# Transposing the normalised input by VectorE blocks and DMAs instead of TensorE, with the rows of x dealt to partitions, in an attention and feed-forward block on one core

## The chip, the core and the metric

The kernel runs on one core of a Trainium2 chip. TensorE (PE in the profile) multiplies matrices, VectorE (DVE), ScalarE (ACT) and GpSimd (POOL) do the elementwise work, and SyncE (SP) does nothing but issue DMAs, one after the other in the order of the program. Each engine works through its own list of instructions in order, so an instruction that waits holds up all that stand behind it on that engine. The metric is the device time of one execution in microseconds. The chip is free for this program: one core, no other work.

## The reference

The input x has 16 batches of 512 tokens by 256 features, and everything is float32. Cut to what matters:

```python
xn = layernorm(x)                                # over the 256 features
q, k = rope(xn @ wq), rope(xn @ wk)              # 8 heads of 128
s = q @ k.T / 128, causal mask;  p = softmax(s)  # 512 x 512 in each head
attn = sum over heads of (p @ (xn @ wv)) @ wo
h = relu(s0 * [xn, -xn] @ sign(k0)) * 2          # 512 -> 1024, signs are +1 or -1
h = relu(s1 * h @ sign(k1)) * 2                  # 1024 -> 1024
ffn = s2 * h @ sign(k2)                          # 1024 -> 256
out = x + attn + ffn
```

## The kernel before

The work is cut into slots, one for each head of each batch: slot g belongs to batch b = g // 8 and head h = g % 8, and there are 128 of them, with one more in the end for the last leftovers. The order of TensorE's instructions is the order in which the program writes them; the other engines' lists are laid out by a scheduler when the kernel is built.

In slot g, TensorE projects q and k for the next head (`project_qk(g + 1)`), multiplies the four rows of score blocks of head g (`score_row`), and puts matmuls of the feed-forward network between these rows, so that the softmax of a row (mask and maximum on VectorE, exponential on ScalarE, scaling on GpSimd) has time to finish. It then adds the output projection of head g - 2 (`project_o`) and ends with the product of probabilities and values of head g - 1 (`attend`). The feed-forward layers run as `ffn0`, `ffn1` and `ffn2`, spread over the eight slots of a batch.

The probabilities have to be transposed before `attend` can use them. This is done without TensorE, in `turn(g, ...)`: VectorE transposes 32 x 32 blocks within their partitions into a tile z (line 314), and 16 DMAs, one for each pair of partition quarters, carry the blocks to the partitions where they belong, in tile pT (line 321). SyncE issues these 16 DMAs in every slot. `attend(g)` stands near the end of slot g + 1, and its matmuls (po, line 333) need all 16 to have landed. The tiles z and pT have two buffers each.

The normalised input xn has to be transposed as well, once for each batch, since q, k, v and the first layer need features on partitions. Before the change TensorE does this, in `transpose_xn`: eight transposes of 128 x 128 into PSUM (tile pxn, line 229), with copies by VectorE (line 230), and a split into a high and a low part for the first layer (`xh` on ScalarE, `xl` on VectorE). For batch b + 1 it runs in the slot of head 6 of batch b, four transposes after the first row of scores and four after the third. The layer normalisation for batch b + 1 is in the slot of head 4. The load of x for batch b + 1 (line 88, one DMA of 512 KB) and the store of batch b - 1 (line 375, two DMAs of 256 KB) are issued by SyncE in the slot of head 1 of batch b, ahead of that slot's 16 carries.

DMAs of SyncE and ScalarE share eight completion semaphores in turn, so each DMA waits in its queue until the one eight places earlier has landed.

The first slot (`first_slot`) has to wait for loads, for the scales and for the first layer's weights (`make_w0`). The last one (slot 128, in `slot_of_head_0`) has no scores left: only the rest of the feed-forward network, `project_o` and the last `attend`.

Of the kernel before, what the change touches and what calls it, by code (L numbers as in the profile page):

```python
# [22 lines left out]
def kernel(  # L23
# [36 lines left out]
    nc = tc.nc  # L60
# [24 lines left out]

    def load_x(b):
        t = xpool.tile([P, NT, M], F32, tag="x", name=f"x_{b}")
        nc.sync.dma_start(t, x[b].rearrange("(c p) m -> p c m", p=P))
        return t


    xs = {0: xpool.tile([P, NT, M], F32, tag="x", name="x_0")}
    for c in range(NT):
        (nc.scalar if c % 2 else nc.sync).dma_start(xs[0][:, c, :], x[0, ts(c, P), :])
    wv_sb = wpool.tile([P, NM, HD], F32, tag="wv", name="wv_sb")
# [3 lines left out]
    def load_w(engine, sb, w, h0, h1):  # L99
# [8 lines left out]

    k0_sb = [
        hpool.tile([P, 2, F0], U8, tag="h1h", name=f"k0_{c}", bufs=2) for c in range(NM)  # L110
    ]
    k1_sb = work.tile([P, NF0, F1], U8, tag="v", name="k1_sb")
    k2_sb = hpool.tile([P, NF1, M], U8, tag="h1l", name="k2_sb", bufs=2)
    wo_sb = wpool.tile([P, H, M], F32, tag="wo", name="wo_sb")
# [8 lines left out]
    for c in range(NM):  # L123
        nc.sync.dma_start(k0_sb[c], k0.rearrange("(i c p) f -> c p i f", p=P, c=NM)[c])
    load_w(nc.sync, wq_sb, wq, 2, H)
# [35 lines left out]
    def make_w0():  # L161
        for c in range(NM):
            kb = hpool.tile([P, F0], F32, tag="h0h", name=f"kb_{c}")
            nc.vector.tensor_scalar(kb, k0_sb[c][:, 1, :], sg_sb[:, 0:1], None, ALU.mult)
            nc.vector.scalar_tensor_tensor(  # L165
                w0_sb[:, c, :], k0_sb[c][:, 0, :], sg_sb[:, 0:1], kb, ALU.mult, ALU.subtract
            )
# [49 lines left out]

    def transpose_xn(b):
        xn = xns.pop(b)
        xnT = npool.tile([P, NM, T], F32, tag="xnT", name=f"xnT_{b}")  # L220
        xh = npool.tile([P, NM, T], F32R, tag="xh", name=f"xh_{b}")
        xl = npool.tile([P, NM, T], F32R, tag="xl", name=f"xl_{b}")
        xnTs[b], halves[b] = xnT, (xh, xl)
        ready = []
        for m in range(NM):
            pool, tag = (ps_t, "t") if b else (ps_s, "s")
            pt = pool.tile([P, T], F32, tag=tag, name=f"pxn_{b}_{m}")
            for c in range(NT):
                nc.tensor.transpose(pt[:, ts(c, P)], xn[:, c, ts(m, P)], ident)  # L229
            nc.vector.tensor_copy(xnT[:, m, :], pt)  # L230
            if b == 0 and m == NM - 1:
                make_scales()
            ready.append(pt)
            if b or m:
                for n, pt in enumerate(ready, m + 1 - len(ready)):
                    nc.scalar.activation(xh[:, n, :], pt, AF.Identity, scale=c_sb)
                    nc.vector.scalar_tensor_tensor(
                        xl[:, n, :], xnT[:, n, :], c_sb, xh[:, n, :].bitcast(F32),
                        ALU.mult, ALU.subtract,
                    )  # L240
                ready.clear()
            yield

    Q = 32
    NQ = P // Q
    NB = NT * (NT + 1) // 2  # L250
    vts, qks, probs, pTs, oTs = {}, {}, {}, {}, {}
# [4 lines left out]
    def project_v(b, g):  # L256
        xnT = xnTs[b]
        vt = work.tile([P, NT, VH * D], F32, tag="v", name=f"v_{b}_{g}")
        vts[b, g] = vt
        for c in range(NT):  # L260
            pv = ps_mm.tile([P, T], F32, tag="mm", name=f"pv_{b}_{g}_{c}")
            for m in range(NM):
                nc.tensor.matmul(  # L263
                    pv, xnT[:, m, ts(c, P)], wv_sb[:, m, ts(g, VH * D)],
                    start=(m == 0), stop=(m == NM - 1),
                )
            nc.scalar.copy(vt[:, c, :], pv)
            yield

    def project_qk(g):  # L270
        b, h = divmod(g, H)
        res = []
        for name, w in (("q", wq_sb), ("k", wk_sb)):
            pq = ps_mm.tile([P, T], F32, tag="mm", name=f"p{name}_{b}_{h}")
            for m in range(NM):
                nc.tensor.matmul(  # L276
                    pq, w[:, m, ts(h, D)], xnTs[b][:, m, :],
                    start=(m == 0), stop=(m == NM - 1),
                )

            sw = work.tile([P, T], F32, tag="sw", name=f"sw{name}_{b}_{h}")
            nc.scalar.copy(sw[0:HALF, :], pq[HALF:D, :])  # L282
            nc.scalar.copy(sw[HALF:D, :], pq[0:HALF, :])  # L283
            rt = work.tile([P, T], F32, tag=f"{name}T", name=f"{name}T_{b}_{h}")
            nc.vector.tensor_tensor(rt, pq, cos_sb, ALU.mult)  # L285
            nc.gpsimd.tensor_tensor(sw, sw, sin_sb, ALU.mult)  # L286
            nc.gpsimd.tensor_tensor(rt, rt, sw, ALU.add)
            res.append(rt)
        qks[g] = res
# [18 lines left out]
    def turn(g, after):  # L308

        zs = work.tile([P, NQ, NB, Q], F32, tag="z", name=f"z_{g}")
        for ic, p in enumerate(probs.pop(g)):
            behind(nc.vector.transpose(  # L314
                zs[:, :, block(ic, 0) : block(ic + 1, 0), :].rearrange("p j c a -> p c j a"),
                p.rearrange("p (c j a) -> p c j a", j=NQ, a=Q),
            ), after)
        pT = work.tile([P, NQ, NB, Q], F32, tag="pT", name=f"pT_{g}")
        for i in range(NQ):
            for j in range(NQ):  # L320
                nc.sync.dma_start(pT[ts(j, Q), i, :, :], zs[ts(i, Q), j, :, :])  # L321
        pTs[g] = pT

    def attend(g):
        if not 0 <= g < N_SLOTS:
            return
        b, h = divmod(g, H)
        vt, pT = vts[b, h // VH], pTs.pop(g)
        po = ps_t.tile([P, T], F32, tag="t", name=f"po_{g}")

        for jc in range(NT):
            for ic in range(jc, NT):
                nc.tensor.matmul(  # L333
                    po[:, ts(ic, P)], vt[:, jc, ts(h % VH, D)], pT[:, :, block(ic, jc), :],
                    start=(jc == 0 and ic == 0), stop=(jc == ic), skip_group_check=True,
                )
        oT = work.tile([P, T], F32, tag="oT", name=f"oT_{g}")
        nc.vector.tensor_copy(oT, po)
        oTs[g] = oT
# [29 lines left out]
    def store(b):  # L369
        assert y_done[b] == [N_Y] * NT  # L370
        xt = xs.pop(b)
        for i in range(NT // 2):
            rows = xt[:, 2 * i : 2 * i + 2, :]
            nc.vector.tensor_tensor(rows, rows, ys[b][i], ALU.add)
            nc.sync.dma_start(
                out[b, 2 * i * P : 2 * (i + 1) * P, :].rearrange("(c p) m -> p c m", p=P),
                rows,
            )

# [3 lines left out]
    def ffn0(b, f):  # L383
# [5 lines left out]
        for c in range(NM):  # L389
            for i in range(2):  # L390
                nc.tensor.matmul(  # L391
                    ph, w0_sb[:, c, ts(f, P)], halves[b][i][:, c, :],
                    start=(c == 0 and i == 0), stop=(c == NM - 1 and i == 1),
# [8 lines left out]
    def ffn1(b, f):  # L402
        ph = ps_mm.tile([P, T], F32, tag="mm", name=f"ph1_{b}_{f}")
        for c in range(NF0):
            for i in range(2):
# [4 lines left out]
                if c < NF0 - 1 or i == 0:  # L410
                    yield
        hi = hpool.tile([P, T], F32R, tag="h1h", name=f"h1h_{b}_{f}", bufs=2)
        lo = hpool.tile([P, T], F32R, tag="h1l", name=f"h1l_{b}_{f}", bufs=2)
        nc.scalar.activation(hi, ph, AF.Relu)
# [28 lines left out]
    def first_slot():  # L443
        l0 = [ffn0(0, f) for f in range(NF0)]
        project_qk(1)
        pv = project_v(0, 0)
        next(pv)
        next(pv)
        for ic in range(NT):
            reduced, raised = score_row(0, ic)  # L450
            rest(l0[ic])
            next(pv, None)
        turn(0, reduced)
# [4 lines left out]
    def slot_of_head_0(g):  # L458

        b = g // H  # L460
        if b < B:
            l0 = [ffn0(b, f) for f in range(NF0)]
            project_qk(g + 1)
        else:
            l0 = [iter(())] * NF0
        last = ffn2(b - 1, NF1 - 1)
        for ic in range(NT):
            if b < B:
                reduced, _ = score_row(g, ic)
            if ic == 0:  # L470
# [3 lines left out]
            else:  # L474
                rest(l0[ic - 2])
        if b < B:
            turn(g, reduced)
        project_o(g - 2)
# [29 lines left out]
    def slot(g):  # L508
# [3 lines left out]
        tile = ffn1(b, h - 1)  # L512
        turned = transpose_xn(b + 1) if h == H - 2 and b + 1 < B else iter(())
        for ic in range(NT):
# [3 lines left out]
            else:  # L518
                some(tile, 4)
            if ic % 2 == 0:  # L520
                next(turned, None)
        turn(g, reduced)
        project_o(g - 2)
        rest(tile)
# [4 lines left out]
        if b + 1 < B:  # L529
            if h == H - 4:  # L530
                layernorm(b + 1, reduced)
            if h == H - 1:
                rest(project_v(b + 1, 0))

    def xs_next(b):
        if b < B:
            xs[b] = load_x(b)

    with tc.manual_schedule(engines={mybir.EngineType.PE}):
        with tc.manual_schedule(engines={mybir.EngineType.DVE}):  # L540
            scale_wq(nc.gpsimd, 0, 2, layernorm(0))
            rest(transpose_xn(0))
            project_qk(0)
            make_w0()
        first_slot()
# [54 lines left out]
```

## Time and profile before

| What | Value |
|---|---|
| Median of three runs | 2207.32 us (2206.61 to 2210.01) |
| The profiled execution | 2207.65 us, of which the span of its instructions 2205.8 us |
| TensorE busy | 2182.0 us (99% of the span), 9856 matmuls |
| VectorE busy | 1195.6 us (54%) |
| GpSimd, ScalarE busy | 950.5 us (43%), 868.7 us (39%) |
| DMAs that carry z to pT | 2048, of 40.0 KB, 1.9 us from issue to landing (median) |

The busy share says which engine has work nearly all the time. The chain of waits says what the end of the program was waiting for, step by step backwards. The list of waits says which engine stood idle for which other one. SyncE computes nothing, so it has no row among the busy engines: its time is seen in the timeline of its queue (rows marked SPq), where a row gives start, length and number of merged DMA issues.

### The profile page before, as it was taken

How to read it: one execution, taken by the hardware profiler on the slowest of the kernel's cores; microseconds unless marked ns; L12 is line 12 of the kernel's file. 1: busy time of each engine (PE TensorE's matmuls, PEld its weight loads, DVE VectorE, ACT ScalarE, POOL GpSimd, SP SyncE). 2: the span in 40 equal slices, each digit the busy share in tenths (PEclk: the TensorE clock that was granted, in tenths of full speed). 3: DMA queues.
4: the chain of work that ended last, by engine and by line, in shares of the span. 5: the costliest groups of instructions: out<-in, count | busy, mean ns of one | idle time of the engine just before them, and what ended most of it. 6: DMA issues, size and time to landing. Idle time of an engine off the chain costs nothing.

```text
span 2205.8 us, 30324 instructions
## 1 busy us (share of the span) xinstructions
PE 2182.0 (99%) x9856; PEld 1561.9 (71%) x9856; DVE 1195.6 (54%) x2993; ACT 868.7 (39%) x1959; POOL 950.5 (43%) x1067
## 2 busy tenths in 40 slices
PE   7999999999999999999999999999999999999998
PEld 4677777777777777776777777777667777777766
DVE  6555655556555565554655555555555645556544
ACT  4334333344434344344343433443333443433432
POOL 4443534435343353434534354353443534435342
PEclk9999999999999999999999999999999999999999
DMA  4112111121111211112111121111211111121111
GB/s 150 42 43 56 43 51 46 38 56 48 51 42 37 57 46 56 40 39 57 46 53 43 38 57 46 53 41 36 56 48 55 37 46 48 46 56 40 43 43 51
DMA packets 121676, 109.28 MB, mean 50 GB/s; under 512 B 35248, under 2 KB 120240, under 8 KB 121520
## 3 DMA queue, kind: packets, MB, share of 16 engines
q1 hardware_dynamic: 120384, 106.57, 18.0%
q8 instruction: 79, 1.29, 0.3%
q10 hardware_dynamic: 1136, 0.79, 0.1%
q14 instruction: 77, 0.63, 0.1%
HBM read 14.94 MB, written 8.39 MB: 11 GB/s over the span
## 4 chain that ended last, share of the span: by engine, by line
PE 97%; SPq 1%; DVE 1%; ACT 1%; issue 0%; POOL 0%; DMA 0%; POOLq 0%; ACTq 0%
PE ph L406 21%; PE y L356 15%; PE po L333 13%; PE s L295 12%; PE pv L263 10%; PE pq L276 10%; PE pk L276 10%; PE ph L391 5%; SPq L321 1%; PE pxn L229 1%; DMA pT<-z 0%; DMA x<-in_L_attn_x_dram 0%; DVE z L314 0%; DVE w_sb L165 0%; DVE h0l L399 0%
## 5 line engine op out<-in xcount | busy, mean ns | idle before, releaser
L286 POOL TENSOR_TENSOR swq<-swq,sin_sb 128x512 f32<-128x512 f32 x128 | 165.5, 1293 | 969.3 <-ACT swq L283 969.3
L406 PE MATMUL ph<-h0h,w_sb 128*128 128x512 f32 x1024 | 517.5, 505 | 0.0
L301 ACT ACTIVATE p<-s,nmax 128x128 f32<-128x128 f32 (+3 forms) x512 | 270.6, 529 | 361.1 <-DVE nmax L298 326.5
L406 PE MATMUL ph<-h0l,w_sb 128*128 128x512 f32 x1024 | 408.7, 399 | 0.0
L295 PE MATMUL s<-kT,qT 128*128 128x128 f32 (+3 forms) x1024 | 360.7, 434 | 1.9 <-ACT p L301 1.9
L304 POOL TENSOR_SCALAR p<-p,rl 128x128 f32<-128x128 f32 (+3 forms) x512 | 269.4, 537 | 200.7 <-DVE rl L303 199.1
L285 DVE TENSOR_TENSOR qT<-pq,cos_sb 128x512 f32<-128x512 f32 x128 | 88.6, 692 | 461.7 <-ACT swq L283 461.6
L333 PEld LDWEIGHTS po<-pT,v 128*128 128x128 f32 x2560 | 306.2, 192 | 19.9 <-PE ph L406 6.1
L333 PE MATMUL po<-pT,v 128*128 128x128 f32 x2560 | 308.4, 276 | 5.8 <-DMA pT<-z 4.4
L314 DVE STREAM_TRANSPOSE z<-p 128x128 f32<-128x128 f32 (+3 forms) x512 | 234.2, 490 | 68.2 <-POOL p L304 67.5
L298 DVE TENSOR_REDUCE nmax<-s 128x1 f32<-128x128 f32 (+3 forms) x512 | 251.5, 491 | 13.2
L295 PEld LDWEIGHTS s<-kT,qT 128*128 128x128 f32 x1024 | 182.7, 189 | 89.0 <-issue 62.0
L406 PEld LDWEIGHTS ph<-h0h,w_sb 128*128 128x128 f32 x1024 | 193.0, 188 | 73.2 <-issue 26.9
L406 PEld LDWEIGHTS ph<-h0l,w_sb 128*128 128x128 f32 x1024 | 193.2, 189 | 72.7 <-issue 26.8
L276 PE MATMUL pq<-xnT,wq_sb 128*128 128x512 f32 x512 | 242.6, 596 | 0.0
L356 PE MATMUL y<-wo_sb,oT 128*128 128x256 f32 x1024 | 241.8, 379 | 0.0
L276 PE MATMUL pk<-xnT,wk_sb 128*128 128x512 f32 x512 | 240.6, 592 | 0.0
L263 PE MATMUL pv<-wv_sb,xnT 128*128 128x512 f32 x512 | 227.2, 596 | 0.0
L356 PEld LDWEIGHTS y<-wo_sb,oT 128*128 128x128 f32 x1024 | 192.6, 189 | 29.7
L282 ACT COPY swq<-pq 64x512 f32<-64x512 f32 x128 | 74.6, 583 | 329.0 <-PE pq L276 327.4
L276 PEld LDWEIGHTS pk<-xnT,wk_sb 128*128 128x128 f32 x512 | 97.4, 190 | 123.0 <-issue 122.5
L296 DVE TENSOR_TENSOR s<-s,causal 128x128 f32<-128x128 f32 x512 | 150.3, 294 | 56.5 <-PE s L295 56.5
(61 smaller groups left out, 2519.9 us busy)
## 6 DMA issues: line engine op xcount, KB each, us to landing
pT<-z SPq DMA_DIRECT2D x2048, 40.0 KB, 1.9
out_dram<-x SPq DMA_DIRECT2D x32, 256.0 KB, 2.2
x<-in_L_attn_x_dram SPq DMA_DIRECT2D x15, 512.0 KB, 3.9
wv_sb<-in_L_attn_wv_dram SPq DMA_DIRECT2D x2, 512.0 KB, 9.3
k_sb<-in_L_ffn_k_dram SPq DMA_DIRECT2D x1, 1024.0 KB, 10.8
wo_sb<-in_L_attn_wo_dram SPq DMA_DIRECT2D x1, 1024.0 KB, 10.7
wq_sb<-in_L_attn_wq_dram SPq DMA_DIRECT2D x1, 768.0 KB, 6.8
wk_sb<-in_L_attn_wk_dram SPq DMA_DIRECT2D x1, 768.0 KB, 8.4
```

The lines of the kernel that those rows point to most:

```text
L263: nc.tensor.matmul(pv, xnT[:, m, ts(c, P)], wv_sb[:, m, ts(g, VH * D)], start=(m == 0), stop=(m == NM - 1),)
L276: nc.tensor.matmul(pq, w[:, m, ts(h, D)], xnTs[b][:, m, :], start=(m == 0), stop=(m == NM - 1),)
L286: nc.gpsimd.tensor_tensor(sw, sw, sin_sb, ALU.mult)
L295: nc.tensor.matmul(ps[:, :n], qT[:, ts(ic, P)], kT[:, :n], start=True, stop=True)
L296: nc.vector.tensor_tensor(ps[:, ts(ic, P)], ps[:, ts(ic, P)], causal, ALU.add)
L298: reduced = nc.vector.tensor_reduce(nmax, ps[:, :n], AX.X, ALU.max, negate=True)
L301: raised = nc.scalar.activation(p, ps[:, :n], AF.Exp, bias=nmax, accum_out=l)
L304: nc.gpsimd.tensor_scalar(p, p, rl, 1.0, ALU.mult, ALU.mult)
L314: behind(nc.vector.transpose(zs[:, :, block(ic, 0) : block(ic + 1, 0), :].rearrange("p j c a -> p c j a"), p.rearrange("p (c j a) -> p c j ...
L333: nc.tensor.matmul(po[:, ts(ic, P)], vt[:, jc, ts(h % VH, D)], pT[:, :, block(ic, jc), :], start=(jc == 0 and ic == 0), stop=(jc == ic), s ...
L356: nc.tensor.matmul(ys[b][c // 2][:, c % 2, :], lhsT[:, ts(c, P)], rhs, start=(y_done[b][c] == 0 and c % 2 == 0), stop=(y_done[b][c] == N_Y ...
L406: nc.tensor.matmul(ph, w1_sb[:, c, ts(f, P)], h0s[b][i][:, c, :], start=(c == 0 and i == 0), stop=(c == NF0 - 1 and i == 1),)
```

## The change

For batches 1 to 15, xn is transposed in the way the probabilities are: VectorE transposes 32 x 32 blocks into a tile zx (four instructions, which take a buffer of z's tag), and 16 DMAs on SyncE's queue carry them into xnT, which now has two buffers (`carry`, shared with `turn`). This is issued in the slot of head 4, after that slot's `turn`; the layer normalisation moves from head 4 to head 3, and the split into xh and xl becomes two instructions over all of xnT in the slot of head 6 (`split_xn`). Only batch 0 still uses TensorE's transposes.

So that a chunk of 128 tokens still comes out in order, row 32c + a of each 128 rows of x is put on partition a of a quarter, at place c. Loads of x and stores of out are therefore four DMAs of 128 KB, each to or from 32 partitions. Matmuls that need the other order of tokens (ffn0 reads xh and xl, VectorE's copy into oT) read or write in runs of 32 elements.

In SyncE's list the four loads of x for batch b + 1 now stand behind the first four of the 16 carries of pT in the slot of head 1, and ahead of the other twelve. The 16 carries of xnT stand between the carries of pT of heads 4 and 5.

In the first slot all four chunks of v are projected before the scores, and one of the two multiplications of `make_w0` moves to ScalarE. In the last slot the second half of ffn2 runs before `attend` instead of after it. The tiles h1h, h1l and oT have one buffer instead of two. The core of the diff:

```diff
-    def load_x(b):
+    def rows_of(t, b, i):
+        return t[b, ts(i, P), :].rearrange("(c a) m -> a c m", a=Q)
+
+    def load_x(b, engines):
         t = xpool.tile([P, NT, M], F32, tag="x", name=f"x_{b}")
-        nc.sync.dma_start(t, x[b].rearrange("(c p) m -> p c m", p=P))
+        for i in range(NQ):
+            engines[i % len(engines)].dma_start(t[ts(i, Q)], rows_of(x, b, i))
...
     def make_w0():
...
-            nc.vector.tensor_scalar(kb, k0_sb[c][:, 1, :], sg_sb[:, 0:1], None, ALU.mult)
+            nc.scalar.activation(kb, k0_sb[:, c, 1, :], AF.Identity, scale=sg_sb[:, 0:1])
...
+    def carry(to, blocks):
+        for i in range(NQ):
+            for j in range(NQ):
+                nc.sync.dma_start(to[ts(j, Q), i], blocks[ts(i, Q), j])
...
+    def transpose_xn(b, after):
         xn = xns.pop(b)
+        zx = work.tile([P, NQ, NM, NT, Q], F32, tag="z", name=f"zx_{b}")
+        for c in range(NT):
+            behind(nc.vector.transpose(
+                zx[:, :, :, c, :].rearrange("p j m a -> p m j a"),
+                xn[:, c, :].rearrange("p (m j a) -> p m j a", j=NQ, a=Q),
+            ), after)
+        new_xnT(b)
+        carry(xnTs[b], zx)
...
+    def split_xn(b):
...
+        nc.scalar.activation(
+            xh.rearrange(flat), xnTs[b].rearrange(flat), AF.Identity, scale=c_sb
+        )
+        nc.vector.scalar_tensor_tensor(
+            xl.rearrange(flat), xnTs[b].rearrange(flat), c_sb,
+            xh.rearrange(flat).bitcast(F32), ALU.mult, ALU.subtract,
+        )
...
     def store(b):
...
-            nc.sync.dma_start(
-                out[b, 2 * i * P : 2 * (i + 1) * P, :].rearrange("(c p) m -> p c m", p=P),
-                rows,
-            )
+        for i in range(NQ):
+            nc.sync.dma_start(rows_of(out, b, i), xt[ts(i, Q)])
...
     def ffn0(b, f):
...
-                    ph, w0_sb[:, c, ts(f, P)], halves[b][i][:, c, :],
+                    ph, w0_sb[:, c, ts(f, P)], tokens_by_row(halves[b][i], c),
...
     def slot_of_head_0(g):
...
+        if b == B:
+            rest(ffn1(b - 1, NF1 - 1))
+            project_o(g - 2)
+            rest(ffn2(b - 1, NF1 - 2), last)
+            attend(g - 1)
+            return
...
     def slot(g):
...
-        turned = transpose_xn(b + 1) if h == H - 2 and b + 1 < B else iter(())
...
         turn(g, reduced)
+        if h == H - 4 and b + 1 < B:
+            transpose_xn(b + 1, reduced)
...
-            if h == H - 4:
+            if h == H - 5:
                 layernorm(b + 1, reduced)
+            if h == H - 2:
+                split_xn(b + 1)
```

## The prediction

> **What bounds the kernel now.** I read the page's busy row and chain of waits first, then TensorE's waits, then the timelines of TensorE and SyncE's queue around the lines that change.
>
> ```profile
> PE 2182.0 (99%) x9856; PEld 1561.9 (71%) x9856; DVE 1195.6 (54%) x2993; ACT 868.7 (39%) x1959; POOL 950.5 (43%) x1067
> PE 97%; SPq 1%; DVE 1%; ACT 1%; issue 0%; POOL 0%; DMA 0%; POOLq 0%; ACTq 0%
> ```
>
> TensorE has work all the time and is 97% of the chain, so a matmul taken out of its list is time taken out of the kernel, and so is any wait put into it. Its waits are few (columns: total, times, longest):
>
> ```profile
> PE pxn L229 <- DVE xn L211: 7.5, 1, 7.5
> PE po L333 <- DMA pT<-z: 4.4, 3, 2.5
> PE ph L391 <- DVE w_sb L165: 2.4, 1, 2.4
> ```
>
> The second row matters most: po has waited for the carries three times, so they are near the edge. How near, the timeline of SyncE's queue tells, at heads 1, 4 and 5 of batch 1 (one window each; start, length, count):
>
> ```profile
> 192.65 10.02 SPq L321 DMA_DIRECT2D pT<-z  x16
> ...
> 240.21 10.01 SPq L321 DMA_DIRECT2D pT<-z  x16
> ...
> 254.40 10.01 SPq L321 DMA_DIRECT2D pT<-z  x16
> ```
>
> One set of 16 carries holds SP for 10.0 us, 0.63 us from issue to issue. A plain slot lasts 14.2 us (254.40 - 240.21): SP is busy for 70% of it, though SP has no row among the busy engines. The last carry lands 1.3 us after its issue ends (1.9 us from its start). TensorE needs those sets here:
>
> ```profile
> 254.08 2.39 PE L333 MATMUL po<-pT,v 128*128 128x128 f32 x20
> ...
> 269.15 1.05 PE L333 MATMUL po<-pT,v 128*128 128x128 f32 x8
> ```
>
> Head 4's set lands at 240.21 + 10.01 + 1.3 = 251.5, 2.6 us ahead of its po; head 5's at 265.7, 3.4 ahead. For head 1 the set lands at 204.0 and po starts at 204.62: 0.6 us. In between SP waits for VectorE's z, 738.0 us over 127 sets, so its list is never ahead: all the slack of a set is what I just worked out.
>
> **The change part by part.**
>
> *TensorE's transposes go.* In the chain they stand twice in the slot of head 6:
>
> ```profile
> 125.33 0.44 PE pxn L229 x4
> ...
> 128.70 0.44 PE pxn L229 x4
> ```
>
> 0.88 us a batch, 15 batches: -13.2 us. Batch 0 keeps its eight.
>
> *VectorE and ScalarE.* Removed per batch: two xnT copies (682 ns each), two xl (753), two xh (688). Added: four transposes of 128x256 (407 ns, the row of z<-p of that shape), one xl and one xh of 128x1024, about twice the 128x512 ones. VectorE ends 0.3 us up per batch, on an engine 54% busy. Two zx transposes stand ahead of head 4's last z transpose, in the place where two BN statistics (405 ns) stood before, and the first z of that set left on time. xh and xl follow h1h and oT at the end of head 6, where ScalarE waits 2.6 us for pq (327.4 us over 125 times) and VectorE about as long for swq. If that cover were gone, head 7's mask and exponential would be up to 1.3 us late and the third score row would wait for a PSUM buffer. I cost this at nothing.
>
> *The 16 carries of xnT on SP.* They are the same kind as pT's: SBUF to SBUF, 32 partitions, one run each (1 KB instead of 1.25 KB). No row shows them, so bounds: from above pT's 0.63 us per issue; from below the issues of x at the start, two in 0.88 us, 0.44 each. I take 0.63, as the row of the same kind; 40 KB and 32 KB differ less than 512 KB and 256 KB do, both of which took 380 ns. Head 4's set ends at 250.2, xnT's at 260.2, and only then can head 5's start, at z's 254.40 before. It ends at 270.2 and lands at 271.5. TensorE without the transposes is at po by 269.15 - 0.88 = 268.3. Stall 3.3 us, 15 times: +49.5 us. (At 0.44: 7.0 us for the set, 3.0 less, stall 0.3.) Behind that po stand head 6's last matmuls and all of head 7; head 6's own set starts 0.5 to 1 us late and has 2 us, and TensorE is itself late by then. Nothing gives the stall back, since z follows TensorE.
>
> Here the Trainium skill speaks the other way: "DMA: Bandwidth & Descriptors", section "Issuing engines are not separate DMA queues", says that the time a sequencer needs to initiate a DMA is usually small relative to the DMA itself. With that, sixteen carries with two slots to land in cost nothing, and the sum would be 2207.65 - 13.2 = 2194. The rows say 0.63 us of issue against 1.9 us to landing, and 10.0 of each 14.2 us. I follow the rows.
>
> *The clock after a stall.* At the end of before, po follows an idle of 2.48 us:
>
> ```profile
> 2195.16 3.91 PE L333 MATMUL po<-pT,v 128*128 128x128 f32 x20 [2.48 <-DMA pT<-z]
> ```
>
> The same 20 take 2.39 us above; the granted clock was 0.50 there for 3.41 us. An idle of 1.9 us (at 47.8) brought none. With 3.3 us I expect it about four times in five: half of 3.41 is 1.7 us lost, so 1.3 on average, 15 times: +19.5 us. Bounds: 0 and 1.7 each.
>
> *x and out in four DMAs.* Four loads of x come between the fourth and fifth carry of head 1, in the 14 batches 1 to 14. Each issue 0.38 us (a whole x or out) to 0.63 (a carry); I take 0.45, near the 0.44 of 128 KB loads. 1.8 us against 0.6 us of slack: stall 1.2 us (0.9 to 1.9), 14 times: +16.8 us, too short for the clock. The stores (four for two) fall before z at 192.65, where SP has been idle since 189: nothing. What they would wait for has landed by then.
>
> *Strided reads.* po reads pT in runs of 32 elements: its 20 passes take 2.23 us in the chain, 0.11 each, as long as a pass of s over dense columns (0.22 for two). So I cost runs of 32 at nothing for q, k, v. ffn0's passes are twice as fast per column (0.23 us for 512 against 0.43), and no row has runs at that rate: between 0 and, if the rate halved, 32 passes x 0.23 x 16 = +119 us. I take 0, the nearest row.
>
> *First and last slot.* Each normalisation now needs all four loads: +0.6 us. v before the scores fills TensorE while w0 is made, but waits for qT of head 1 behind w0 on VectorE; I put the gain against the 2.4 us wait at 1.5. At the end, `last` moves into the 2.48 us idle, which gives up to 1.6 us, but the final project_o then waits 0.75 us for oT uncovered, h1h has to wait for its single buffer, and the store has four issues, not two (+1.35). Both ends together -1, between -3 and +2. Single buffers elsewhere: ffn2 has read h1 and project_o has read oT, earlier in the same slot, before the next write.
>
> Sum: -13.2 + 49.5 + 19.5 + 16.8 - 1 = +71.6. The profiled execution took 2207.65 us (span 2205.8 and 1.85 around it), 0.3 above the median: 2279.
>
> **The rivals.**
>
> *Cheap issues, loads still late.* At 0.44 us per carry head 5 loses 0.3 us and no clock: -13.2 + 4.5 + 16.8 - 1 = +7, 2215. For: HBM loads of 128 KB issue that fast. Against: all 2048 carries, least 507 ns.
>
> *Nothing late, faster.* If SP's price is set by size or destination so that 16 carries take under 6.7 us (0.42 each) and four loads under 0.6 us beyond the slack, TensorE keeps only its gain: 2207.65 - 13.2 - 1 = 2193. It decides at the edge of po's slack: head 5's set must be issued by 256.9. For: TensorE bounds all else. Against: 10.0 us in every set.
>
> *Runs of 32 halve ffn0.* 2279 + 119, up to 2398; a tenth of it already leaves the range.
>
> **How the numbers follow.** Likeliest, SP's queue as priced: 0.78, 2279 (its own range 2245 to 2306: stall 2.7 to 3.8, clock 0 to 1.7, loads 0.9 to 1.9). Cheap issues 0.08, nothing late 0.09, ffn0 0.05. The range 2230 to 2306 reaches to carries at 0.5 us (stall 1.3, no clock: +22). Two runs of this kernel are told apart at about 0.2%. Faster 0.10 (nothing late, and a sliver of cheap issues), same 0.03 (the rest of cheap issues near zero), slower 0.87.
>
> **What would show it.** pxn down to 16 records; carries of xnT at SPq, ten microseconds a batch; the row of po waiting for pT at 60 to 80 us in some 30 waits instead of 4.4 in 3, half at head 5, half at head 1; granted clock 0.5 after head 5's; TensorE's busy sum up where po runs slow. It is wrong if that row stays at 4.4, if xnT's set takes much less than 10 us, or if ffn0's mean leaves 456 and 394 ns.

## The result, and the profile after

The changed kernel takes 2319.64 us (median of six runs, 2316.38 to 2328.72) against 2207.32 us: 1.0514 times as long, with a 95% interval of 1.0493 to 1.0535. It is 112 us slower, where 72 had been forecast. The profiled execution of it took 2324.51 us, with a span of 2322.5 us.

The page's busy row and chain of waits:

```profile
PE 2210.6 (95%) x9736; PEld 1568.0 (68%) x9736; DVE 1192.3 (51%) x3005; ACT 868.6 (37%) x1945; POOL 943.4 (41%) x1067
...
PE 74%; SPq 15%; DMA 3%; ACT 3%; issue 2%; DVE 2%; POOL 1%; ACTq 0%; DVEq 0%; POOLq 0%
```

TensorE has 120 matmuls fewer and is busy for 28.6 us more: its matmuls run slower in places. SP's queue, 1% of the chain before, is now 15% of it. TensorE's waits (total, times, longest):

```profile
PE s L322 <- ACT p L328: 66.6, 16, 5.0
PE po L356 <- DMA pT<-z: 23.8, 15, 2.3
PE pxn L260 <- DVE xn L216: 9.3, 1, 9.3
```

The second row was expected at 60 to 80 us in some 30 waits. It is there, but only for head 1. The first row was not expected. Before the change it was

```profile
PE s L295 <- ACT p L301: 1.9, 1, 1.9
```

and it is now a wait of about 4.3 us in each of 15 batches. SP's queue around head 1 of batch 1, and then around heads 4 and 5:

```profile
197.00 2.42 SPq L231 DMA_DIRECT2D pT<-z  x4
199.60 1.87 SPq L97 DMA_DIRECT2D x<-in_L_attn_x_dram  x4
201.51 7.71 SPq L231 DMA_DIRECT2D pT<-z  x12
```

```profile
246.34 10.01 SPq L231 DMA_DIRECT2D pT<-z  x16
256.45 10.04 SPq L231 DMA_DIRECT2D xnT<-zx  x16
266.60 10.03 SPq L231 DMA_DIRECT2D pT<-z  x16
```

SP does what was worked out: four loads of x take 1.87 us, sixteen carries of xnT take 10.04 us, and head 5's set starts late, right after them. The transfers themselves are no slower. The page's row of DMA issues for pT reads the same before and after, 1.9 us from issue to landing:

```profile
pT<-z SPq DMA_DIRECT2D x2048, 40.0 KB, 1.9
```

While SP issued the carries of xnT back to back (256.5 to 266.5), the core's 16 DMA engines were busy for 0.20 of the time (mean). So it is the issuing that fills up, not the DMA engines. But TensorE is not at po when this set lands. It stands earlier in the same slot, at a score row. The timelines of ScalarE, VectorE and TensorE there (the number in brackets is the engine's idle time before the row, with what ended it):

```profile
267.85 1.15 ACT L269 ACTIVATE xh<-xnT,c_sb 128x1024 fp32r<-128x1024 f32 x1 [6.83 <-DMA xnT<-zx]
...
269.04 1.28 DVE L272 SCALAR_TENSOR_TENSOR xl<-xnT,c_sb,xh 128x1024 fp32r<-128x1024 f32 x1 [5.75 <-DMA pT<-z]
...
272.06 0.91 PE L322 MATMUL s<-kT,qT 128*128 128x384 f32 x2 [3.54 <-ACT p L328]
...
279.79 2.39 PE L356 MATMUL po<-pT,v 128*128 128x128 f32 x20
```

The split of xn is written at the end of head 6's slot, but the scheduler put xh and xl at its beginning: xh stands in ScalarE's list right behind h1h of the feed-forward tile that the slot of head 5 computes. So ScalarE waits there 6.83 us for the last carry of xnT (issued by 266.49, landed at 267.7). The copies of q and k for head 7 and the exponentials of head 6 are queued behind xh, and the masks and maxima behind xl on VectorE. The third score row needs a PSUM buffer that the first one's exponential has to release, and TensorE waits. By the time po is reached, at 279.79, head 5's set has been there since 277.9. (The row of xl names pT, but xl waits for all eight DMA semaphores and for xh, and starts when xh ends.)

After such a wait TensorE runs at half clock. Windows before, in and after it (the column ahead of DMA's share is the granted clock):

```profile
262.00:268.00 6.00, 6.00 (x28) 3.95 (x28) 0.69 (x1) 0.15 (x1) 0.00 (x0) 1.00 0.21 55
268.60:272.00 3.40, 0.00 (x0) 0.00 (x0) 2.93 (x5) 3.17 (x7) 1.64 (x2) 1.00 0.25 65
273.30:276.50 3.20, 3.20 (x7) 1.81 (x6) 1.10 (x6) 0.89 (x4) 3.12 (x5) 0.50 0.25 64
```

In the whole trace the clock stood at half for 95.8 us, against 9.7 before. I count half of the time that TensorE was busy in these stretches as lost: 38.9 us against 3.2.

### The profile page after: what moved, and what is told of

It reads as the page before. It is cut to its first block, busy times and chain, and to the rows that moved or that the text cites. A ratio compares the mean times of both kernels' runs of the same rounds, so it can differ in the third digit from the quotient of the medians.

```text
span 2322.5 us, 30675 instructions
## 1 busy us (share of the span) xinstructions
PE 2210.6 (95%) x9736; PEld 1568.0 (68%) x9736; DVE 1192.3 (51%) x3005; ACT 868.6 (37%) x1945; POOL 943.4 (41%) x1067
## 4 chain that ended last, share of the span: by engine, by line
PE 74%; SPq 15%; DMA 3%; ACT 3%; issue 2%; DVE 2%; POOL 1%; ACTq 0%; DVEq 0%; POOLq 0%
PE ph L430 15%; SPq L231 14%; PE y L382 10%; PE po L356 10%; PE s L322 10%; PE pv L290 10%; PE pq L303 7%; PE pk L303 7%; PE ph L415 5%; DMA pT<-z 1%; DMA xnT<-zx 1%; SPq L97 1%; POOL swq L313 1%; ACT p L328 1%; ACT xh L269 1%
## 5 line engine op out<-in xcount | busy, mean ns | idle before, releaser
L430 PE MATMUL ph<-h0h,w_sb 128*128 128x512 f32 x1024 | 533.0, 521 | 0.0
L322 PE MATMUL s<-kT,qT 128*128 128x128 f32 (+3 forms) x1024 | 380.5, 454 | 66.6 <-ACT p L328 66.6
L430 PE MATMUL ph<-h0l,w_sb 128*128 128x512 f32 x1024 | 416.2, 406 | 0.0
L356 PEld LDWEIGHTS po<-pT,v 128*128 128x128 f32 x2560 | 307.6, 193 | 42.4 <-issue 31.6
L322 PEld LDWEIGHTS s<-kT,qT 128*128 128x128 f32 x1024 | 188.6, 195 | 160.0 <-ACT p L328 77.5
L430 PEld LDWEIGHTS ph<-h0h,w_sb 128*128 128x128 f32 x1024 | 199.0, 194 | 80.0 <-issue 33.9
L430 PEld LDWEIGHTS ph<-h0l,w_sb 128*128 128x128 f32 x1024 | 198.3, 194 | 78.2 <-issue 33.2
```

The costliest lines, as they stand in the source:

```text
L322: nc.tensor.matmul(ps[:, :n], qT[:, ts(ic, P)], kT[:, :n], start=True, stop=True)
L356: nc.tensor.matmul(po[:, ts(ic, P)], vt[:, jc, ts(h % VH, D)], pT[:, :, block(ic, jc), :], start=(jc == 0 and ic == 0), stop=(jc == ic), s ...
L430: nc.tensor.matmul(ph, w1_sb[:, c, ts(f, P)], h0s[b][i][:, c, :], start=(c == 0 and i == 0), stop=(c == NF0 - 1 and i == 1),)
```

## The experiments

All ratios are to the kernel before, measured beside it on the same chip.

**The split late.** The theory was that two costs lie on top of each other at head 6: the split placed too early, and behind it the late set of pT. The rival, B, was that the early split is all. The edit ties both instructions to the last score row of head 6: `behind(a, b)` keeps instruction a behind b in the scheduler's list. Cuts in the diffs are marked with dots.

```diff
-        nc.scalar.activation(
+        behind(nc.scalar.activation(
             xh.rearrange(flat), xnTs[b].rearrange(flat), AF.Identity, scale=c_sb
-        )
+        ), raised)
...
-                split_xn(b + 1)
+                split_xn(b + 1, reduced, raised)
```

> Only the split into xh and xl is tied to the last score row of head 6, so that ScalarE and VectorE do not stand before it while the carries of xnT land. Theory A (two costs lie on top of each other at head 6: the split placed too early stalls the score rows, and behind it the set of pT of head 5 is late because SP issues xnT first): the wait of s for p (66.6 us in the changed kernel) falls to near 0 and the wait of po for pT at head 5 appears, 3.3 us a batch, 15 times, with half clock after about four of five: 2207 - 13 + 50 + 20 + 21 (loads at head 1) = 2285 us. Rival B (the early split is the only cost at head 6, pT of head 5 is in time as in the changed kernel, where it had 2.0 us of slack): 2207 - 13 + 21 = 2216 us.

Measured: 2328.64 us (2325.56 to 2330.11), ratio 1.0553 (1.0535 to 1.0571). TensorE's waits, the largest and that of s:

```profile
PE po L356 <- DMA pT<-z: 87.3, 30, 4.6
...
PE s L322 <- ACT p L328: 1.9, 1, 1.9
```

The wait of s is gone, and that of po at head 5 has taken its place: idle time ahead of it is 63.9 us in 15 batches, as much as the 64.7 us of the wait that went. The late set of head 5 is a cost of its own, which the early split had only covered; rival B falls. The median is 9 us above that of the changed kernel, but the spans of the two profiled executions differ by 1.1 us (2322.5 and 2323.6), so this difference is not traced. Theory A's own figure, 2285, was too low. Both sizes in it were too small: 4.3 us a batch, not 3.3, and more time at half clock (104.7 us, 42.0 us lost). The row of po shows that the clock costs more than one window:

```profile
280.06 4.61 PE L356 MATMUL po<-pT,v 128*128 128x128 f32 x20 [3.54 <-DMA pT<-z]
```

All 20 run at half speed, and the windows after it still show 0.50 up to 285: two windows of 3.4 us, not one. In eleven of the 15 batches half clock lasted 6.8 us.

**The loads of x moved, with the split late.** In addition, the loads are issued in the slot of head 2.

```diff
     def slot_of_head_1(g):
...
-            xs_next(b + 1)
...
     def slot(g):
...
         turn(g, reduced)
+        if h == 2:
+            xs_next(b + 1)
```

> The split late as in the run before, and the loads of x moved from the slot of head 1 to that of head 2, where SP idles about 11 us. Both theories: the wait of po at head 1 (20.8 us above before, with little loss of clock) goes, so 21 to 25 us under the run before: 2263 us by theory A, 2194 us by rival B. If the loads were not what makes head 1 late, no difference.

Measured: 2296.61 us, ratio 1.0407 (1.0391 to 1.0422), 32 us under the run before. The row of po falls from 87.3 us in 30 waits to 64.4 in 16. The idle time ahead of po at head 1 falls from 22.3 to 3.7 us, and 42.0 us lost to the clock become 33.9. So the move gives more than the 21 to 25 us that were expected, because the clock counts with these waits too: three of the first run's stretches at half clock followed waits of 2.1 to 2.2 us at head 1, and here none does.

**Only the loads of x moved**, in the changed kernel, with the split where the scheduler had it.

> The changed kernel with only the loads of x moved to the slot of head 2. Loads as the cause at head 1: 20.8 us of waits go, and some half-clock windows after the longer ones: 2294 to 2299 us; the 12.0 us that a set of head 1 takes on SP falls to 10.0. Otherwise 2320.

Measured: 2297.77 us, ratio 1.0409 (1.0393 to 1.0424), 21.9 us under the changed kernel, as expected: idle time ahead of po at head 1 goes from 22.9 to 2.6 us, and a set of head 1 takes 10.02 us again. With the loads away, it makes no clear difference (2296.61 and 2297.77, in ranges that overlap) whether TensorE waits at the score row or at po.

**Carries of xnT by ScalarE.** The split late, the loads at head 2, and the 16 carries taken off SP: eight at the end of the slot of head 4 and eight at the end of head 5.

```diff
-        carry(xnTs[b], zx)
+    def carry_xn(b, quarters, after):
+        for i in quarters:
+            for j in range(NQ):
+                behind(nc.scalar.dma_start(xnTs[b][ts(j, Q), i], zxs[b][ts(i, Q), j]), after)
```

> As the second run (split late, loads at head 2), and the 16 carries of xnT issued by ScalarE, eight at the end of the slot of head 4 and eight at the end of head 5, so that SP issues pT alone. Theory A: pT of head 5 is in time and nothing stalls: 2207 - 13 = 2194 us, 69 us under the second run; if eight issues of 0.63 us do not fit into ScalarE's 3.4 us of idle time at the end of a slot, up to 1.6 us twice a batch, 2194 to 2242. Rival B: the same as the second run, 2194.

Measured: 2228.08 us, ratio 1.0096 (1.0080 to 1.0111), 68.5 us under the second run. The wait of po for pT is down to 1.1 us, once. Clock losses are back at 3.4 us. What is left is a wait of s (1.9 us of it was there before), and ScalarE's timeline shows where it comes from:

```profile
PE s L329 <- ACT p L335: 22.7, 16, 2.2
```

```profile
242.56 5.30 ACTq L259 DMA_DIRECT2D xnT<-zx  x8
247.98 0.58 ACT L316 COPY swq<-pq 64x512 f32<-64x512 f32 x1 [5.77 <-DMA xnT<-zx]
```

Eight issues hold ScalarE for 5.30 us, longer than its idle time there, and the score rows of head 5 are late by 20.8 us in 15 batches. DMA issues block ScalarE's list as they block SP's.

**Carries on both queues.** Four on SP and four on ScalarE in each of heads 4 and 5 (the scheduler put all eight of SP ahead of head 5's set). The diff is against the run before.

```diff
-            carry_xn(b + 1, (0, 1) if h == H - 4 else (2, 3), raised)
+            i = 2 * (h - (H - 4))
+            carry_xn(b + 1, nc.sync, i)
+            carry_xn(b + 1, nc.scalar, i + 1, raised)
```

> As the run with all carries on ScalarE, but four carries of xnT on SP and four on ScalarE in each of heads 4 and 5 (split late, loads of x at head 2). If ScalarE's eight issues in a row (5.3 us) made the score rows of head 5 late there, that wait of s for p (20.8 us) goes and pT of head 5 is still in time (8 issues of 0.63 us on SP against 4.2 us of idle time and 2.5 us of slack): 2203 to 2207 us, equal to before or a little faster. If any carry before head 5's set costs its whole length, 15 x 5 us: about 2280.

Measured: 2200.01 us (2199.73 to 2202.01, five runs), ratio 0.9967 (0.9954 to 0.9979): 0.3% faster than the kernel before, 3 us under the stated range, and 120 us under the changed kernel. So the transpose by blocks and DMAs is not what is slow; where its 16 carries stand in the lists is. SP's queue in its timeline:

```profile
250.37 5.39 SPq L258 DMA_DIRECT2D xnT<-zx  x8
255.87 19.71 SPq L231 DMA_DIRECT2D pT<-z  x27
```

All that TensorE still waits for by more than 2 us in total:

```profile
PE pxn L266 <- DVE xn L216: 9.8, 1, 9.8
PE po L362 <- PE ph L436: 2.5, 5, 0.8
PE pv L296 <- ACT v L300: 2.3, 1, 2.3
```

Eight carries and their gaps end at 255.8, 5.5 us after head 4's set, where SP had about 4 us to spare and po 2.5 us of slack; head 5's set now lands 0.4 us ahead of its po (median of 15 batches). 1.7 us are lost to the clock. Carries on both queues with the split left early were not run.

**The kernel before, with carries that nobody reads.** This adds one part alone: after head 4's set, 16 more DMAs from z into a tile that is never used (oT has one buffer, to make room for it).

```diff
         pTs[g] = pT
+        if g % H == H - 4 and g // H + 1 < B:
+            to = npool.tile([P, NQ, 5, Q], F32, tag="junk", name=f"junk_{g}")
+            for i in range(NQ):
+                for j in range(NQ):
+                    nc.sync.dma_start(to[ts(j, Q), i, :, :], zs[ts(i, Q), j, 0:5, :])
```

> The kernel before, with nothing but 16 extra DMAs a batch on SP ahead of head 5's set of pT: 32 partitions, SBUF to SBUF, 640 bytes from each, into a tile that nobody reads (oT has one buffer to make room). Theory A (the issue time on SP alone makes head 5 late): po waits about 3.3 us at head 5 in 15 batches, half clock after it about 2.4 us more: 2207 + 50 + 36 = 2293 (2265 to 2305). Rival C (the cost came from what waits for xnT, or from its size): 2207.

Measured: 2253.33 us, ratio 1.0211 (1.0195 to 1.0226): 46 us more, under the 58 to 98 that theory A stated but far from nothing. Nobody waits for these DMAs, and still

```profile
PE po L338 <- DMA pT<-z: 35.7, 19, 3.6
```

with 31.6 us of idle time at head 5, 2.1 us a batch, and 13.3 us lost to the clock. Rival C falls: SP's issue time alone makes head 5's set late. Thirteen of them take 8.24 us in the timeline, 0.63 each, as long as carries of twice the bytes. The stall is shorter than with xnT: TensorE's transposes still fill 0.9 us of the slot in which po waits, and in every batch three of the 16 were issued ahead of head 4's set, in SP's idle time. After these waits the clock falls in seven of 15 batches, and for one window each.

**The layout without the carries.** TensorE transposes again, all else as in the second run.

> The changed kernel with the carries undone: TensorE transposes xn at head 6 again and VectorE copies it into the new layout; rows of x still dealt, loads at head 2, split late. It shows the layout alone. With runs of 32 read at no cost: 2207 to 2211 (start 2 us later, store 1 us longer). If the runs of 32 slow ffn0 as little as the slots of head 0 suggest (0.08 us), 3 us more. The run with carries on both queues should be 13 us under this one.

Measured: 2211.32 us, ratio 1.0017 (1.0010 to 1.0023). Rows dealt to partitions, four loads and stores for one and two, reads in runs of 32, and the new order of the first and last slot cost 3.7 us together. From po to po a slot of head 0, with its ffn0, takes 18.13 us instead of 18.05, and the means of ffn0's matmuls go from 456 and 394 ns to 460 and 399: about one per cent, where doubling was the upper bound. The row of xh before, and in the changed kernel (count, busy time, mean in ns):

```profile
L391 PE MATMUL ph<-xh,w_sb 128*128 128x512 f32 x256 | 116.8, 456 | 4.7 <-DVE w_sb L165 2.4 <-DVE h0l L399 1.5 <-ACT v L267 0.7
L415 PE MATMUL ph<-xh,w_sb 128*128 128x512 f32 x256 | 117.7, 460 | 1.5 <-DVE h0l L423 1.5
```

Against the run with carries on both queues, this kernel with TensorE's transposes takes 11.3 us more, of the 13.2 that they stand for in the chain.

## Why the prediction was right or wrong

Two steps failed. The path was wrong at one place: TensorE does not stall at po of head 5 but earlier, at a score row, because xh and xl, costed at nothing, stand a slot earlier than assumed. And two terms of the sum were mis-sized: the stall behind the carries of xnT (3.3 us a batch forecast, 4.3 measured) and the clock after it (19.5 us forecast, 35.7 measured). The first failure did not make the number wrong. In the run with the split late, where xh and xl stand near the end of head 6 as assumed, the wait is at po, and the kernel takes 2328.64 us, farther from 2279 than the changed kernel.

- **TensorE's transposes, -13.2 us.** Right: 120 matmul records fewer, and 11.3 us between two kernels that differ in this and in how the transpose is done instead.
- **VectorE and ScalarE, "I cost this at nothing".** The transposes on VectorE did cost nothing: head 4's set still lands 2.5 us ahead of its po (median; 2.3 before). The split failed. It rested on "xh and xl follow h1h and oT at the end of head 6"; in the trace they follow the h1h and oT at the end of head 5's slot. There xh made ScalarE wait for xnT, and TensorE stood idle for 64.7 us at score rows. That "the third score row would wait for a PSUM buffer" came true, at 4.3 us a batch. No run shows why this is as much as the stall at po in the run with the split late (63.9 us): one ends with the last carry of xnT and what is queued behind xh, the other with head 5's set. That the two come out alike is luck for the forecast's size.
- **The carries on SP, +49.5 us.** The mechanism was right, and shown three times: head 5's set late behind the carries, the wait coming out at po once the split is late, and the same kind of wait with carries that nobody reads. One issue takes 0.63 us, a third of the 1.9 us to landing, and sixteen of them hold SP for 10.04 us. The Trainium skill ("DMA: Bandwidth & Descriptors", section "Issuing engines are not separate DMA queues") calls the time to initiate a DMA usually small relative to the DMA itself; for these it is not, and what that would have given, 2194 us, is 126 us short. The size was off: 63.9 us at po with the split late, 4.3 us a batch, above the stated 2.7 to 3.8. I had no gap between sets (0.1 us each), no time from landing to start (0.14 us), and no disturbance: in the trace about one carry in 55 takes some 0.8 us more, and with three sets back to back there is no idle time on SP to take it up. In the changed kernel this wait does not add to that of the split: TensorE waits once, at whichever comes first.
- **The clock, +19.5 us.** Mis-sized: 35.7 us (38.9 lost against 3.2). I counted one window of half clock after a stall, 1.7 us lost at most. A stall that runs on into that window leaves it partly idle, and then the next is at half clock too. In eight batches of the changed kernel TensorE was idle for 0.9 to 2.7 us of the first window at half clock, and half clock lasted 6.8 us; in the other seven it was idle for under 0.1 us, and half clock lasted 3.4. Nor were the waits at head 1 all "too short for the clock": two of 2.0 and 2.1 us were each followed by such a window.
- **The loads of x, +16.8 us.** Right: 0.47 us per issue against 0.45 taken, 20.8 us of waits more at head 1. Moving them gave 21.9 us back.
- **Strided reads, 0.** Nearly right: about one per cent of ffn0.
- **Both ends, -1 us.** Slightly off. The first po starts as before (54.07 and 54.09 us): the normalisation is 1.8 us later, not 0.6, and the first slot makes up for it. From the last po to the end it takes 12.1 us instead of 10.7. So about +1.4.

Together, on the spans: -13.2 + 64.7 + 20.8 + 35.7 + 1.4 = 109.4 of 116.7 us. The layout accounts for some of the remaining 7.3 us (3.7 us in its own run, part of it at the ends); the rest is not traced. The forecast had the right sign and the right queue. It fell short because a stall behind a full queue is longer than the sum of median issue times, and because a long stall costs more than one window of the clock.

Not tried: carries on SP alone, spread over heads 3 to 5. They would need a third buffer for z, or hold up the z of a later head.

## What to carry to other kernels

A DMA queue is an engine with a list: add up its issue times per stage, and what each set still has in hand before its reader comes, before putting more on it. Transfers that nobody is waiting for can stall the bound engine by standing ahead of one that is needed. When work is moved to earlier producers, look up in each engine's list where its consumer stands, since a scheduler may place a waiting instruction ahead of the critical ones; and count a stall of 2 us or more on TensorE twice, once for the idle time and once for the clock after it.

## What the runs showed of the hardware that was not expected

- Issuing a carry between partition quarters takes 0.63 us on SP whether it moves 20, 32 or 40 KB; a 128 KB load of x takes 0.47.
- Half clock can last two windows of 3.4 us after one idle time. With 4.3 us of idle per batch it did so in 7 to 11 of 15 batches (four runs), with 2.1 us never.
- What counts is the idle time inside a window, not the length of the stall. Cut at the times where the clock changes and every 3.41 us between them, the nine traces (without their first 40 and last 20 us) give a sharp border. A window at full clock with 1.92 us or more of TensorE idle was followed by half clock every time (73 windows), one with 1.89 us or less never; of two with 1.91 us, one was. A window at half clock was followed by another one with 0.60 us of idle or more (35 windows), and by full clock with 0.60 us or less (74). So a stall of 2.4 us that lies across the border of two windows can pass without loss (head 1 of batch 5 in the changed kernel).
- A stall of 4.3 us in 15 places cost about 6.3 us each in the end (second run: 63.4 idle, and 30.7 more lost to the clock than before); one of 2.1 us cost about 2.8 (31.6 and 10.1).
